# A Nyström block with inverses in one chain, changed to two chains of inverses with a shorter beginning

## The chip, the core and the metric

The kernel runs on one core of a Trainium2 chip. The core has TensorE (PE, matmuls; the weight loads are listed apart as PEld), VectorE (DVE), ScalarE (ACT), GpSimd (POOL) and SyncE (SP, which issues DMAs). Matmuls write to PSUM; DVE and ACT empty it. The metric is the device time of one execution in microseconds (us), lower is better.

## The reference

Sixteen batches of 1024 rows of 256 go through a Nyström attention (16 heads of width 16, 64 landmarks) and then an expert network, each with a layer norm before it, one behind it, and a residual.

```python
def iterative_inv(K, n_iter=6):
    denom = jnp.max(jnp.sum(K, axis=-2), axis=-1)[:, :, None, None]
    V = jnp.swapaxes(K, -1, -2) / denom
    for _ in range(n_iter):
        KV = jnp.matmul(K, V)
        V = jnp.matmul(0.25 * V, 13 * I - jnp.matmul(KV, 15 * I - jnp.matmul(KV, 7 * I - KV)))
    return V
...
Q_l, K_l = means of Q and K over each 16 rows          # 64 landmarks
kernel1 = softmax(Q @ K_l.T); kernel2 = softmax(Q_l @ K_l.T); kernel3 = softmax(Q_l @ K.T)
SV = (kernel1 @ iterative_inv(kernel2)) @ (kernel3 @ V);  out = SV @ w_proj
...
base = x @ W_base + b_base
h = relu(x @ Wd1[e] + bd1[e]);  recon = h @ Wd2[e] + bd2[e]      # 8 experts
idx = argmin over e of mean((recon - x) ** 2)
out = base + relu(x @ Wa_down[idx] + ba_down[idx]) @ Wa_up[idx] + ba_up[idx]
```

kernel2 is a 64x64 matrix per head; its inverse is the iteration above, a long chain of small products. All arithmetic is float32.

## The kernel before

The work of a batch is cut into stages. Stage a (`stage_a`, L322) transposes the normalized rows, makes Q, K and V (L351, L372), the landmark means `lm` (L392) and `bd` (L395; the means of a pair of heads side by side, zero elsewhere), then the weights of kernel3 (L420, L444, L455), their product with V (L483), normalized to `u` (L536). Stage p (`stage_p`, L540) makes kernel2, inverts it and multiplies the inverse with `u` into `w_bd` (L733, L735). Stage c (`stage_c`, L740) makes the weights of kernel1 (L766, L795, L804, L812), multiplies them with `w_bd` (L833), projects (L881) and writes x1. Stage d1 (`stage_d1`, L932) norms x1, runs the eight experts (L954, L987; differences `df` at L995, their squares on ACT at L998), picks the best one and gathers its weights by DMA; stage d2 (`stage_d2`, L1061) computes the output (L1070, L1088, L1089).

Stage p in detail. Eight tiles of 64 columns on 128 partitions hold the 16 matrices. `kp` (L596, four DVE instructions) is the landmark means with all but one pair of heads masked to zero, by `pairmask`; two products of 256 columns with all 128 rows give the scores `pk` (L600). Maximum, difference, exp, sum, reciprocal and product (L608 to L617) make kernel2. A product with `eye` transposes it (L577, `pkt`), L625 sums its columns (`cs`). A transpose of `cs` (L628, `pcs`), maximum and reciprocal over 8 partitions (L630, L632), a copy `rrow` (L634), a transpose back (L637, `prd`) and a copy (`rd`, L639) bring each head's reciprocal denominator to all of its partitions, and `vi` (L641) is the first V. Of the six iterations every second one (0, 2, 4) begins with a product `pkv` of kernel2 and `vi`, each has `psq`, `pb` and a last product (`px` or `pvi`), all made by the helper `product` at L577, 64x64 pieces, 32 records for 16 heads and one product; each step waits for DVE or ACT to turn the step before into the next operand (L653, L655, L692, L698, L662, L683, L707, L723, L725). In iteration 0 a second product with `eye` gives the transposed copy `vt` of `vi` (L577, `pkv<-eye,vi`, and L686). `across` (L658) copies half of the operand y to the other 64 partitions.

The order of the work is not that of the code. Each stage is a generator that yields, before each piece of work, a name, the names that it follows, and the estimated costs on PE, DVE and ACT. Four streams, one per stage kind, each go through the batches 0 to 15 in turn: a, p, c, d1 with d2. A planner (`planned`, L1244) puts the pieces of all streams in one order by a model of the engines: at each point it tries each stream's next piece, looks 70 us ahead (250 us from the end it looks to the end) by simple rules, and takes what loses the least PE time. The rules prefer the stream with the lowest progress: its rank (0 for a, 1 for p, 2 for c, 3 for d) plus the share of its work done, times 16. The order is then fixed for PE, ACT, DVE and POOL; each of them works through its own queue in that order.

What ties the streams: p needs `bd` of its batch; the `bd` step of a (which overwrites `lm`, one buffer) follows `kp` of the batch before; `weighted` of c follows the end of p; Q has three buffers, so a follows c three batches earlier; x1 has two, so c follows d two batches earlier; `u` and `w_bd` have two each. The tiles of p (`mat`, L550) have one buffer each. PSUM is four slots of two banks (`two_banks`, `one_bank` both take one slot), shared by all streams. Large work tiles come from `buf4k` (L106): `df` has three buffers of tag `df`, the normed rows `xn_d` (L942) and the output y_d (L301) two of tag `yd`. The two bias rows that are loaded at the start lie in buffers of `df`. In stage d2 POOL sets three rows of `a_t` (L1065, L1066), issued between the step `a`'s go-ahead and its products.

## Time and profile before

| | |
|---|---|
| median of 10 executions | 2368.16 us (2363.08 to 2371.74) |
| profiled execution, its own time | 2364.72 us |
| its span, first to last instruction | 2362.9 us |
| granted TensorE clock, mean | 0.98 |
| PE, DVE, ACT busy | 2162.4, 1424.4, 1317.1 us |
| DMA | 60.36 MB, 26 GB/s on average |

In a line of groups, "x512" is the count, "238.2, 608" the union of busy time in us and the mean duration in ns of one, and behind the bar stands the idle time of the engine just before these instructions with what ended it; "issue" means that the trace shows nothing that was waited for. PE's records overlap each other, so count times mean is more than busy time. In a line of waits the three numbers are the total, the number of times and the longest, in us. In a line of stretches come the stretch, its length, the busy time of PE, PEld, DVE, ACT and POOL with counts, the granted clock as a share of full speed, the DMA share and GB/s.

### The profile page before, as it was taken

How to read it: one execution, taken by the hardware profiler on the slowest of the kernel's cores; microseconds unless marked ns; L12 is line 12 of the kernel's file. 1: busy time of each engine (PE TensorE's matmuls, PEld its weight loads, DVE VectorE, ACT ScalarE, POOL GpSimd, SP SyncE). 2: the span in 40 equal slices, each digit the busy share in tenths (PEclk: the TensorE clock that was granted, in tenths of full speed). 3: DMA queues.
4: the chain of work that ended last, by engine and by line, in shares of the span. 5: the costliest groups of instructions: out<-in, count | busy, mean ns of one | idle time of the engine just before them, and what ended most of it. 6: DMA issues, size and time to landing. Idle time of an engine off the chain costs nothing.

```text
span 2362.9 us, 85848 instructions
## 1 busy us (share of the span) xinstructions
PE 2162.4 (92%) x39346; PEld 1382.3 (58%) x39346; DVE 1424.4 (60%) x2715; ACT 1317.1 (56%) x2659; POOL 271.7 (12%) x387
## 2 busy tenths in 40 slices
PE   7999989999899999999999999999999999898965
PEld 4666565565655656566565656657556465655442
DVE  6546565756457666666656657575656656474633
ACT  2345655645655556564656646575554655666635
POOL 1001020110200202010020201102010020101021
PEclk9999999999999999999999999999999999999978
DMA  3000001010010100101010100101001010000000
GB/s 112 20 21 21 2 22 39 5 56 2 14 46 3 58 3 16 44 5 56 2 58 2 37 23 3 57 2 59 1 5 56 2 40 2 14 29 24 18 21 21
DMA packets 56626, 60.36 MB, mean 26 GB/s; under 512 B 4996, under 2 KB 55240, under 8 KB 56264
## 3 DMA queue, kind: packets, MB, share of 16 engines
q1 hardware_dynamic: 50240, 50.35, 6.8%
q8 instruction: 309, 5.06, 0.9%
q0 software_dynamic: 2560, 2.14, 0.3%
q10 hardware_dynamic: 3464, 2.37, 0.3%
q14 instruction: 53, 0.43, 0.1%
HBM read 38.08 MB, written 16.78 MB: 23 GB/s over the span
## 4 chain that ended last, share of the span: by engine, by line
PE 43%; DVE 8%; ACT 7%; issue 3%; POOL 1%; DMA 0%; POOLq 0%; DVEq 0%; ACTq 0%
PE ph L954 6%; PE pq L351 5%; PE pr L987 4%; PE pf L1088 4%; PE po L881 3%; ACT df L998 3%; PE pf L1089 2%; DVE df L995 2%; PE pv L372 2%; PE psv L833 2%; PE psct L804 2%; PE psct L812 1%; PE put L483 1%; PE psm L420 1%; PE pb L577 1%
## 5 line engine op out<-in xcount | busy, mean ns | idle before, releaser
L998 ACT ACTIVATE df<-df,bd_sb 128x512 f32<-128x512 f32 x512 | 363.2, 711 | 128.9 <-DVE df L995 128.0
L995 DVE TENSOR_TENSOR df<-pr,xt_d 128x1024 f32<-128x1024 f32 x256 | 302.7, 1217 | 85.0 <-PE pr L987 50.4
L987 PE MATMUL pr<-ht,wd_sb 64*64 64x512 f32 x2048 | 252.3, 597 | 6.7 <-ACT e L822 2.4
L954 PE MATMUL ph<-xt_d,wd_sb 128*128 128x512 f32 x512 | 238.2, 608 | 1.0 <-ACT e L822 0.7
L351 PE MATMUL pq<-xt_a,wqkv_sb 128*128 128x512 f32 x512 | 230.0, 599 | 0.0
L429 DVE TENSOR_REDUCE mx<-psm 128x2 f32<-128x1024 f32 x128 | 149.9, 1216 | 46.2 <-PE psm L420 45.9
L774 DVE TENSOR_REDUCE maxima<-psc 128x16 f32<-128x1024 f32 x128 | 150.1, 1215 | 28.0 <-PE psc L766 28.0
L954 PEld LDWEIGHTS ph<-xt_d,wd_sb 128*128 128x128 f32 x512 | 93.7, 192 | 115.9 <-issue 97.8
L822 ACT ACTIVATE e<-psct 128x1024 f32<-128x1024 f32 x128 | 123.4, 1015 | 66.2 <-PE psct L812 64.3
L351 PEld LDWEIGHTS pq<-xt_a,wqkv_sb 128*128 128x128 f32 x512 | 94.2, 190 | 108.2 <-issue 102.6
L465 ACT ACTIVATE e<-psc 128x1024 f32<-128x1024 f32 x128 | 122.5, 1021 | 32.4 <-PE psc L455 32.2
L1088 PE MATMUL pf<-wbase_sb,xt_d 128*128 128x256 f32 x512 | 137.6, 392 | 1.3 <-ACT xx L683 1.3
L881 PE MATMUL po<-wproj_sb,svt 128*128 128x256 f32 x512 | 120.6, 389 | 7.2 <-ACT vt L707 3.6
L260 POOL TENSOR_SCALAR ve_c_y<-ss_c 128x4 f32<-128x4 f32 x32 | 6.2, 194 | 1023.6 <-ACT square_c L306 1023.3
L692 DVE TENSOR_TENSOR sq<-psq,eye 128x512 f32<-128x512 f32 x96 | 65.8, 686 | 94.3 <-PE psq L577 90.9
L295 DVE SCALAR_TENSOR_TENSOR y_d<-y_d,rstd_d_y,x 128x256 f32<-128x256 f32 x128 | 53.2, 479 | 110.7 <-POOL rstd_d_y L262 110.7
L698 DVE TENSOR_TENSOR t<-eye,pb 128x512 f32<-128x512 f32 x96 | 65.4, 681 | 89.7 <-PE pb L577 89.5
L987 PEld LDWEIGHTS pr<-ht,wd_sb 64*64 64x64 f32 x2048 | 64.6, 133 | 89.3 <-issue 47.9
L372 PE MATMUL pv<-wqkv_sb,xt_a 128*128 128x256 f32 x512 | 116.6, 382 | 0.2 <-ACT e L822 0.2
L962 ACT ACTIVATE ht<-ph,bd_sb 128x1024 f32<-128x1024 f32 x64 | 70.9, 1108 | 74.8 <-PE ph L954 74.4
L881 PEld LDWEIGHTS po<-wproj_sb,svt 128*128 128x128 f32 x512 | 96.5, 193 | 25.9 <-ACT svt L856 4.8
L1088 PEld LDWEIGHTS pf<-wbase_sb,xt_d 128*128 128x128 f32 x512 | 97.9, 194 | 18.5 <-issue 3.4
(183 smaller groups left out, 4118.4 us busy)
## 6 DMA issues: line engine op xcount, KB each, us to landing
out_dram<-y_d SPq DMA_DIRECT2D x32, 512.0 KB
x<-in_L_attn_x_dram SPq DMA_DIRECT2D x15, 1024.0 KB
xa<-in_L_attn_x_dram SPq DMA_DIRECT2D x15, 1024.0 KB
xa<-in_L_attn_x_dram SPq DMA_DIRECT2D x2, 512.0 KB
x<-in_L_attn_x_dram SPq DMA_DIRECT2D x2, 512.0 KB
wqkv_sb<-in_L_attn_w_qkv_dram ACTq DMA_DIRECT2D x1, 768.0 KB
wd_sb<-in_L_ffn_Wd_dram ACTq DMA_DIRECT2D x2, 256.0 KB
wd_sb<-in_L_ffn_Wd_dram ACTq DMA_DIRECT2D x1, 512.0 KB
```

The source lines that it names most:

```text
L351: nc.tensor.matmul(pq[:, n, :], lhsT=wqkv_sb[:, k, f0 : f0 + P], rhs=xt[:, k, n * 512 : (n + 1) * 512], start=(k == 0), stop=(k == NC - 1),)
L372: nc.tensor.matmul(pv[:, j, :], lhsT=xt[:, k, (t0 + j) * P : (t0 + j + 1) * P], rhs=wqkv_sb[:, k, 2 * D : 3 * D], start=(k == 0), stop=(k ...
L429: nc.vector.tensor_reduce(mx3[:, n, q : q + 2], psc[g], X, ALU.max)
L465: nc.scalar.activation(e, psc[g], AF.Exp)
L774: nc.vector.tensor_reduce(mx[:, t0 : t0 + 2, 64 * g : 64 * g + 64].rearrange("x t (p j) -> x p t j", p=2)[:, :, :, 0 : 2 * NC], psc[g].rea ...
L822: nc.scalar.activation(e, psc[g], AF.Exp)
L881: nc.tensor.matmul(po[:, j, :], lhsT=svt[n][:, c, j * P : (j + 1) * P], rhs=wproj_sb[:, c, :], start=(c == 0), stop=(c == NC - 1),)
L954: nc.tensor.matmul(ph[:, n, :], lhsT=wd1_sb[:, k, 2 * i : 2 * i + 2, :].rearrange("p e h -> p (e h)"), rhs=xt[:, k, n * 512 : (n + 1) * 51 ...
L987: nc.tensor.matmul(pr[to, r, :], lhsT=wd2_sb[half, i, k * P + 64 * f : k * P + 64 * f + 64], rhs=ht[half, cols], start=True, stop=True,)
L995: nc.vector.tensor_tensor(df, pr, middle(xt[:, k, cols], 2), ALU.subtract)
L998: nc.scalar.activation(df[:, r, :], df[:, r, :], AF.Square, bias=bd2_sb[:, e, k : k + 1], accum_out=part[:, e, k * NW + n : k * NW + n + 1],)
L1088: nc.tensor.matmul(po[:, j, :], lhsT=xt[:, k, cols], rhs=wbase_sb[:, k, :], start=(k == 0), stop=False)
```

## The change

Stage p begins differently. Each pair of heads has its scores from a product of 32 rows and 64 columns, straight from `lm` (no `kp`, no `pairmask`), into four PSUM banks, two slots; maximum and difference are done for each slot. One product of kernel2 with `in_half` (ones in each 64x64 diagonal block) gives the sums of the columns on every partition of a head; maximum and reciprocal follow directly, `rd` needs no transposes. V in the transposed layout, `vt`, is kernel2 times `rd`; `vi` isn't made, since the first `pkv` is the product of kernel2's transpose with itself, scaled by `rd` on DVE as `xh`, and y is made from `xh`. `across` stores only the half that is read.

Stage p is split into two streams, for even and odd batches, both of rank 1, and its tiles have one buffer for each parity. A stream's progress is now its rank plus the batch plus the done share of that batch. `bd` follows the step `k2` instead of `kp`. `xn_d`, `df` and `y_d` share one pool of four buffers (tag `yd`); the bias rows lie in buffers of `e1`, and stage c of batch 0 follows their use. The memsets of `a_t` are issued in the last step of d1.

```diff
@@ -133,9 +133,9 @@
     nc.scalar.dma_start(out=wbase_sb, in_=w_base.rearrange("(k p) f -> p k f", p=P))
-    bd1_rows = work.tile([E // 2, P], F32, tag="df", name="bd1_rows", bufs=3)
+    bd1_rows = work.tile([E // 2, P], F32, tag="e1", name="bd1_rows")
     nc.scalar.dma_start(out=bd1_rows, in_=bd1.rearrange("(i r) h -> i (r h)", r=2))
-    bd2_rows = work.tile([E * NC, P], F32, tag="df", name="bd2_rows", bufs=3)
+    bd2_rows = work.tile([E * NC, P], F32, tag="e1", name="bd2_rows")
@@ -156,6 +156,10 @@
     nc.gpsimd.memset(ones, 1.0)
+    in_half = const.tile([P, P], F32, name="in_half")
+    nc.gpsimd.memset(in_half, 0.0)
+    for _, half in halves():
+        nc.gpsimd.memset(in_half[half, half], 1.0)
@@ -165,7 +169,6 @@
-    pairmask = groups("pairmask", PC)
@@ -298,7 +301,7 @@
-        y = buf4k(tag, [P, 4, D], f"y_{at}{b}_{h}")
+        y = buf4k(tag, [P, 4, D], f"y_{at}{b}_{h}", 4 if tag == "yd" else 2)
@@ -383,7 +386,7 @@
                     ("a", b, "bd"),
-                    [("a", b, "qk", i, c) for i in range(2) for c in range(NC)] + ([("p", b - 1, "kp")] if b >= 1 else []),
+                    [("a", b, "qk", i, c) for i in range(2) for c in range(NC)] + ([("p", b - 1, "k2")] if b >= 1 else []),
@@ -548,7 +551,7 @@
         def mat(tag, name=None):
-            return inv.tile([P, NP, M], F32, tag=tag, name=f"{name or tag}_{b}")
+            return inv.tile([P, NP, M], F32, tag=f"{tag}{b % 2}", name=f"{name or tag}_{b}")
@@ -573,7 +576,11 @@
                         assert rows_y == rows
-                        yt = y[h[y_at[0]] ^ h[y[2]]] if isinstance(y, tuple) else y
+                        yt = y
+                        if isinstance(y, tuple) and h[y_at[0]] != h[y[2]]:
+                            yt, j = y[1], 2 * (j // 4) + j % 2
+                        elif isinstance(y, tuple):
+                            yt = y[0]
@@ -588,58 +595,60 @@
-        yield step("kp", ew("dve", 0.8, None))
+        yield step(
+            "k2",
+            mm(0.15, "r32", 16),
+            mm(0.15, "r32", 16),
+            *(ew("dve", 0.4, 1) for _ in range(3)),
+            ew("dve", 0.4, 1, "free"),
+            ew("act", 0.5, -1, "free"),
+        )
         lm, bd = live[b].pop("lm"), live[b]["bd"]
-        kp = inv.tile([P, NC, PC, M], F32, tag="yx", name=f"kp_{b}")
-        for p in range(PC):
-            nc.vector.tensor_scalar(kp[:, :, p, :], lm[:, 1], pairmask[:, p : p + 1], None, ALU.mult)
-        yield step("k2", mm(1.3, "full", 8), ew("dve", 1.25, -1, "free"), ew("act", 0.5))
-        pk = one_bank([P, NP, M], f"pk_{b}")
+        pk = [two_banks([P, 2, 512], f"pk_{b}_{g}") for g in range(PC // 2)]
         for c in range(NC):
-            nc.tensor.matmul(
-                pk[:, c * PC : (c + 1) * PC, :].rearrange("x p l -> x (p l)"),
-                lhsT=bd[:, c, :, :].rearrange("f r l -> f (r l)"),
-                rhs=kp[:, c].rearrange("f p l -> f (p l)"),
-                start=True,
-                stop=True,
-            )
-        mx = small.tile([P, NP], F32, tag="mx2", name=f"mx2_{b}", bufs=1)
-        nc.vector.tensor_reduce(mx, pk, X, ALU.max)
+            for p in range(PC):
+                nc.tensor.matmul(
+                    pk[p // 2][:, p % 2, c * M : (c + 1) * M],
+                    lhsT=bd[rows32(p), c, :, :].rearrange("f r l -> f (r l)"),
+                    rhs=lm[rows32(p), 1, c, :],
+                    start=True,
+                    stop=True,
+                )
+        mx = small.tile([P, NP], F32, tag=f"mx2{b % 2}", name=f"mx2_{b}", bufs=1)
         k2 = mat("vt", "k2")
-        nc.vector.tensor_tensor(k2, pk, last(mx, M), ALU.subtract)
+        for g in range(PC // 2):
+            scores = pk[g][:, :, 0 : NC * M].rearrange("x p (c m) -> x p c m", c=NC)
+            most = mx.rearrange("x (c g p) -> x g p c", c=NC, g=2)[:, g]
+            nc.vector.tensor_reduce(most, scores, X, ALU.max)
+            nc.vector.tensor_tensor(
+                k2.rearrange("x (c g p) m -> x g p c m", c=NC, g=2)[:, g], scores, last(most, M), ALU.subtract
+            )
...
         yield step("k2n", ew("dve", 1.5, None))
-        sm = small.tile([P, NP], F32, tag="sm2", name=f"sm2_{b}", bufs=1)
+        sm = small.tile([P, NP], F32, tag=f"sm2{b % 2}", name=f"sm2_{b}", bufs=1)
         nc.vector.tensor_reduce(sm, k2, X, ALU.add)
-        rs = small.tile([P, NP], F32, tag="rs2", name=f"rs2_{b}", bufs=1)
+        rs = small.tile([P, NP], F32, tag=f"rs2{b % 2}", name=f"rs2_{b}", bufs=1)
...
         nc.vector.tensor_tensor(k2, k2, last(rs, M), ALU.mult)
-        yield step("k2t", mm(Q, "q64", 64), ew("act", 0.5, -1, "free"), ew("dve", 0.6))
...
+        yield step(
+            "k2t", mm(0.9, "full", 4), mm(Q, "q64", 64), ew("dve", 0.85, 0, "free"), ew("act", 0.5, 1, "free"), ew("dve", 0.6, None, "aside")
+        )
+        pcs = one_bank([P, NP, M], f"pcs_{b}")
+        nc.tensor.matmul(
+            pcs.rearrange("x q m -> x (q m)"), lhsT=in_half, rhs=k2.rearrange("x q m -> x (q m)"), start=True, stop=True
+        )
...
         kt_at = product(pkt[0], (k2, NATURAL), (eye, None), "t", ("p2", "s"))
+        cs = small.tile([P, NP], F32, tag=f"cs{b % 2}", name=f"cs_{b}", bufs=1)
+        nc.vector.tensor_reduce(cs, pcs, X, ALU.max)
+        rd = small.tile([P, NP], F32, tag=f"rd{b % 2}", name=f"rd_{b}", bufs=1)
+        nc.vector.reciprocal(rd, cs)
...
-        cs = small.tile([P, NP], F32, tag="cs", name=f"cs_{b}", bufs=1)
-        nc.vector.tensor_reduce(cs, k2t, X, ALU.add)
-        yield step("rrow", mm(0.2, "full", 4), ew("dve", 0.6, -1, "free"))
-        pcs = one_bank([NP, 2, M], f"pcs_{b}")
-        nc.tensor.transpose(pcs.rearrange("q r m -> q (r m)"), cs, ident)
-        cmx = small.tile([NP, 2], F32, tag="cmx", name=f"cmx_{b}", bufs=1)
-        nc.vector.tensor_reduce(cmx, pcs, X, ALU.max)
-        rmx = small.tile([NP, 2], F32, tag="rmx", name=f"rmx_{b}", bufs=1)
-        nc.vector.reciprocal(rmx, cmx)
-        rrow = inv.tile([NP, 2, M], F32, tag="yc", name=f"rrow_{b}")
-        nc.vector.tensor_copy(rrow, last(rmx, M))
-        yield step("v0", mm(0.1, "full", 2), ew("act", 0.15, -1, "free"), ew("dve", 0.6))
-        prd = one_bank([P, NP], f"prd_{b}")
-        nc.tensor.transpose(prd, rrow.rearrange("q r m -> q (r m)"), ident[:NP, :NP])
-        rd = small.tile([P, NP], F32, tag="rd", name=f"rd_{b}", bufs=1)
-        nc.scalar.copy(rd, prd)
-        vi = mat("vi")
-        nc.vector.tensor_tensor(vi, k2t, last(rd, M), ALU.mult)
-        v_at = kt_at
+        vt, vt_at = k2, NATURAL
+        nc.vector.tensor_tensor(vt, k2, last(rd, M), ALU.mult)
@@ -656,34 +665,36 @@
         def across(y):
-            other = mat("yc", "across")
-            frm, to = (t.rearrange("x (f k p) m -> x f k (p m)", f=2, k=2) for t in (y, other))
+            other = inv.tile([P, NP // 2, M], F32, tag=f"yc{b % 2}", name=f"across_{b}")
+            frm, to = y.rearrange("x (f k p) m -> x f k (p m)", f=2, k=2), other.rearrange("x (f p) m -> x f (p m)", f=2)
             for r, half in halves():
-                nc.scalar.copy(to[64 - 64 * r : 128 - 64 * r, :, r, :], frm[half, :, 1 - r, :])
+                nc.scalar.copy(to[64 - 64 * r : 128 - 64 * r], frm[half, :, 1 - r, :])
...
             if i % 2 == 0:
-                n = 2 if i == 0 else 1
...
                     f"kv{i}",
-                    mm(n * Q, "q64", 64 * n),
-                    ew("dve", 0.6, 0),
-                    ew("act", 0.5, 0, "aside" if i == 0 else "free aside"),
-                    *([ew("act", 0.5, 0, "free aside")] if i == 0 else []),
+                    mm(Q, "q64", 64),
+                    ew("dve", 0.6, 0, "free" if i == 0 else ""),
+                    ew("dve", 0.6) if i == 0 else ew("act", 0.5, 0, "free aside"),
...
                 )
-                px, pvt = banks_of(f"pkv{i}")
-                x_at = product(px, (k2t, kt_at), (vi, v_at), h, (g, "p2"))
+                px, _ = banks_of(f"pkv{i}")
+                first = (k2t, kt_at) if i == 0 else (vi, v_at)
+                x_at = product(px, (k2t, kt_at), first, h, (g, "p2"))
                 if i == 0:
-                    vt_at = product(pvt, (vi, v_at), (eye, None), h, (g, "p2"))
-                y = taken_y(px, 1.0)
-                xh = mat("xx")
-                nc.scalar.copy(xh, px)
-                if i == 0:
-                    vt = mat("vt")
-                    nc.scalar.copy(vt, pvt)
+                    xh, y = mat("xx"), mat("yx")
+                    by_pair, rd_by_pair = px.rearrange("x (u p) m -> x u p m", p=2), rd.rearrange("x (p u) -> x u p", p=2)
+                    nc.vector.tensor_tensor(
+                        xh.rearrange("x (u p) m -> x u p m", p=2), by_pair, last(rd_by_pair, M), ALU.mult
+                    )
+                    nc.vector.tensor_tensor(y, xh, middle(eyes[0], NP), ALU.subtract)
+                else:
+                    y = taken_y(px, 1.0)
+                    xh = mat("xx")
+                    nc.scalar.copy(xh, px)
@@ -741,7 +752,7 @@
         w_bd = w_bds[b % 2]
-        first = [("a", b, "bd"), *([("d", b - 2, "end")] if b >= 2 else [])]
+        first = [("a", b, "bd"), *([("d", 0, "weights")] if b == 0 else []), *([("d", b - 2, "end")] if b >= 2 else [])]
@@ -939,7 +950,7 @@
         def dst(h):
-            xns[h] = buf4k("yd", [P, 4, D], f"xn_d{b}_{h}")
+            xns[h] = buf4k("yd", [P, 4, D], f"xn_d{b}_{h}", 4)
@@ -991,7 +1002,7 @@
                             )
-                    df = buf4k("df", [P, 2, 512], f"df_{b}_{i}_{k}_{n}", 3)
+                    df = buf4k("yd", [P, 2, 512], f"df_{b}_{i}_{k}_{n}", 4)
@@ -1056,14 +1067,14 @@
         centre(wup)
-        live[b].update(xt=xt, wdn=wdn, bdn=bdn, wup=wup)
...
-    def stage_d2(b):
-        xt, wdn, bdn, wup, x1 = (live[b].pop(k) for k in ("xt", "wdn", "bdn", "wup", "x1"))
-        yield go(("d", b, "a"), [("d", b, "wup")], mm(1.72, "c64", 16), ew("act", 1.0, -1, "free"))
...
         nc.gpsimd.memset(a_t[R : R + 2, :], 0.5)
+        live[b].update(xt=xt, wdn=wdn, bdn=bdn, wup=wup, a_t=a_t)
...
+    def stage_d2(b):
+        xt, wdn, bdn, wup, x1, a_t = (live[b].pop(k) for k in ("xt", "wdn", "bdn", "wup", "x1", "a_t"))
+        yield go(("d", b, "a"), [("d", b, "wup")], mm(1.72, "c64", 16), ew("act", 1.0, -1, "free"))
@@ -1098,15 +1109,21 @@
-    def chain(stages):
-        for b in range(NB):
+    def chain(stages, batches=range(NB)):
+        for b in batches:
...
-    RANKS = 0, 1, 2, 3
+    RANKS = 0, 1, 1, 2, 3
     def streams():
-        return [chain(stages) for stages in ([stage_a], [stage_p], [stage_c], [stage_d1, stage_d2])]
+        return [
+            chain([stage_a]),
+            chain([stage_p], range(0, NB, 2)),
+            chain([stage_p], range(1, NB, 2)),
+            chain([stage_c]),
+            chain([stage_d1, stage_d2]),
+        ]
@@ -1123,11 +1140,17 @@
     for rank, stream in zip(RANKS, stretches):
-        sums = [0.0]
-        for _, _, parts in stream:
-            sums.append(sums[-1] + sum(p[1] for p in parts if p[0] == "pe"))
+        sums, of_batch = [0.0], [0.0] * (NB + 1)
+        at, stream_progress = {}, []
+        for (_, b, *_), _, parts in stream:
+            of_batch[b] += sum(p[1] for p in parts if p[0] == "pe")
+        for (_, b, *_), _, parts in stream:
+            us = sum(p[1] for p in parts if p[0] == "pe")
+            at[b] = at.get(b, 0.0) + us
+            stream_progress.append(rank + b + (at[b] - us) / max(of_batch[b], 1.0))
+            sums.append(sums[-1] + us)
         before.append(sums)
-        progress.append([rank + NB * at / sums[-1] for at in sums])
+        progress.append(stream_progress)
...

```

## The prediction

> **What bounds the kernel now.** I read the page's totals first, then TensorE's groups by shape, then TensorE's waits, then the order in time around one inverse, then the last quarter millisecond in stretches.
>
> The page's totals, before:
>
> ```profile
> span 2362.9 us, 85848 instructions
> PE 2162.4 (92%) x39346; PEld 1382.3 (58%) x39346; DVE 1424.4 (60%) x2715; ACT 1317.1 (56%) x2659; POOL 271.7 (12%) x387
> ```
>
> TensorE (PE) is the bound; VectorE (DVE) and ScalarE (ACT) have 40% of their time free. So a microsecond of PE work is worth about a microsecond, work on the others is worth something only where PE waits for it. PE's groups by shape (busy us, mean ns | idle before):
>
> ```profile
> L954 PE MATMUL ph<-xt_d,wd_sb 128*128 128x512 f32 x512 | 238.2, 608 | 1.0 <-ACT e L822 0.7
> L766 PE MATMUL psc<-bd,qt 32*128 32x128 f32 x2048 | 81.7, 285 | 5.6 <-DVE t L698 2.3 <-DVE mx L429 1.3 <-DVE maxima L774 0.6
> L577 PE MATMUL psq<-yx 64*64 64x64 f32 x3072 | 67.7, 224 | 11.4 <-DVE yx L653 4.4 <-DVE yx L655 1.9 <-issue 1.8
> L577 PE MATMUL pb<-yx,sq 64*64 64x64 f32 x1536 | 65.3, 223 | 16.4 <-DVE sq L692 8.8 <-ACT e L822 6.3 <-ACT vt L707 0.6
> L577 PE MATMUL pkv<-vi,k2t 64*64 64x64 f32 x1536 | 34.9, 228 | 5.6 <-issue 2.6 <-ACT vi L723 2.1 <-DVE vi L641 0.6
> L600 PE MATMUL pk<-kp,bd 128*128 128x256 f32 x64 | 17.6, 397 | 1.2 <-DVE kp L596 0.7 <-DVE u L536 0.3 <-ACT e L822 0.2
> L577 PE MATMUL pkv<-eye,vi 64*64 64x64 f32 x512 | 11.1, 221 | 1.9 <-issue 1.9
> L628 PE MATMUL pcs<-ident,cs 128*8 128x128 f32 x16 | 4.4, 272 | 3.4 <-DVE cs L625 3.4
> L637 PE MATMUL prd<-ident,rrow 8*128 8x8 f32 x16 | 3.3, 208 | 0.5 <-DVE df L995 0.4
> ```
>
> Matmuls overlap, so the price of one is busy time over count, not the mean: 0.465 us for L954's 512 columns. Each product in the code leaves two records, a transpose one. PE's waits, the rows that matter here:
>
> ```profile
> PE pb L577 <- DVE sq L692: 8.8, 10, 1.8
> PE pf L1089 <- POOL a_t L1066: 8.3, 5, 3.8
> PE pb L577 <- ACT e L822: 6.3, 7, 1.8
> PE psq L577 <- DVE yx L653: 4.4, 5, 1.7
> PE po L881 <- ACT vt L707: 3.6, 2, 2.0
> ```
>
> The first and fourth are the inverse waiting for its own last step. The third and fifth are another thing: pb reads no e, so there PE waited for a PSUM slot that ScalarE was emptying. DVE's order in time where one inverse gives way to the next (start, us):
>
> ```profile
> 1244.66 0.86 DVE L596 TENSOR_SCALAR kp<-lm,pairmask 128x128 f32<-128x128 f32 x4
> 1245.56 0.29 DVE L392 TENSOR_SCALAR lm<-lsum 128x256 f32<-128x256 f32 x1
> ...
> 1264.81 0.69 DVE L641 TENSOR_TENSOR vi<-k2t,rd 128x512 f32<-128x512 f32 x1 [4.34 <-ACT rd L639]
> ```
>
> kp of batch 9 (counted from 0) is followed at once by lm of batch 10: stage a of the next batch stood ready and waited for an inverse to begin, and an inverse begins when the one before ends. The instructions of kp run from 38.3 (first) to 2082.9 (last of 16 batches), (2082.9 - 38.3) / 15 = 136 us apart, while one inverse takes 159.8 - 38.3 = 121 us (first) and 2184.3 - 2082.9 = 101 us (last) from kp to its product pw. The one chain of inverses is nearly always under way. The end, in stretches (PE busy, granted clock after POOL):
>
> ```profile
> 2140.00:2170.00 30.00, 23.34 (x490) 17.29 (x485) 10.94 (x31) 13.90 (x31) 7.92 (x9) 0.94 0.03 7
> 2170.00:2200.00 30.00, 23.21 (x476) 18.32 (x476) 17.91 (x41) 12.68 (x29) 4.81 (x8) 0.83 0.22 72
> 2230.00:2264.00 34.00, 26.22 (x381) 14.04 (x379) 16.14 (x36) 22.15 (x53) 7.30 (x9) 0.89 0.02 6
> ```
>
> **The change part by part.** The sum is against the profiled execution, 2364.7 us (span 2362.9), 3.4 below the median of ten, 2368.2.
>
> *PE work out.* pk 17.6 + the transposed copy of vi 11.1 + pcs 4.4 + prd 3.3 = 36.4 us, all on PE.
>
> *PE work in.* The product with in_half has 512 columns, one per batch, 32 records at L954's 0.465 = 14.9 us. The scores by pairs are 8 products of 64 columns on 32 rows per batch, 256 records. L766 (32 rows, 128 columns) costs 81.7 / 2048 = 0.040, so at most 10.2; by half the columns 5.1; by 64-column pkv, 34.9 / 1536 = 0.023, 5.8. I take 6, since pkv has the same columns. Net -36.4 + 20.9 = -15.5 (ends -11 and -16). The Trainium skill, "TensorEngine Tiling (Array Packing)", section Restrictions and Gotchas, speaks against this part: row tiles need different PSUM banks at the same time, so the step holds more PSUM. The code does hold two slots of four where pk held one; by the rule the step's gain of 11.6 (17.6 - 6) would be given back in waits, a sum of 2326.
>
> *Steps out.* The two visits of PE for pcs and prd go with their waits, 3.4 + 0.5, and the 1.2 before pk is traded for a like wait: -4 (ends 0 and -7).
>
> *VectorE and ScalarE.* Out on DVE: kp 13.8, cmx 4.4, rmx 2.4, rrow 3.4 = 24.0. In: rd 16 x 0.203 = 3.2; xh by a multiplication 16 x 0.686 = 11.0; maxima and subtraction in halves, 64 of 0.419 (L493, 128x256) = 26.8 for 22.1 now. Net -5. ACT loses rd 2.6, vt 9.5 and 16 xx copies of 0.583 = 21.4. Both lie beside PE's work: 0. Where the cover is gone, in the chain of one inverse, kp to vi took 1264.81 + 0.69 - 1244.66 = 20.8 us; kp (0.86), the rrow operations (0.27 + 0.15 + 0.21) and the wait for rd (4.34) go, xh before y adds 0.69, so about 5 us per inverse, which only the chain feels.
>
> *Two streams.* The idle before all L577 groups except the removed one sums to 11.4 + 16.4 + 2.7 + 5.6 + 4.4 + 0.8 + 6.5 + 7.0 + 1.3 = 56.1 us. In it 14.6 are "issue", which stays, and about 10.5 waits for a PSUM slot; 31 are waits of one inverse for itself. With the other inverse at another step these have cover: ends 0 (both always wait together) and -31. I take -18, some three fifths, because another chain is close behind: stage c of a batch waits for stage d two batches earlier (x1 has two buffers), and stage c and d of one batch span about 261 us (batch 9: from its first scores at 1376 to its last output at 1637), 131 per batch against the inverse's 136. PE's idle is 2362.9 - 2162.4 = 200.5 us, 12 of it after its last matmul (2351); before other products it is thus 132. Start (14.5), last batch (11.2 + 5.3 + 7.9), a_t (8.3), issue (about 22) and the steps out (7) leave 56, of which a further ready product may fill a seventh: -8 (ends 0 and -56).
>
> *Against that.* Two inverses hold PSUM slots while the engines empty them. The waits for slots in PE's list sum to about 45 us over the span; I add a quarter, +10 (ends 0 and +70, the rival).
>
> *The end.* In 2140 to 2264 PE is busy 23.3 + 23.2 + 29.7 + 26.2 = 102.5 of 124, idle 21.5; the clock's missing shares (0.06 x 30 + 0.17 x 30 + 0.11 x 34) are 10.6 more. In that time the last inverse is alone on its chain and ends at 2185, though its bd was written at 1958 and the stage c before ended at 2163. With two streams it is done before. But stage c of batch 15 also waits for stage d of batch 13, which ends at 2182, so that is what is late next. I take -8 (ends 0 and -32). After 2264 stage d of the last batch is alone, ScalarE's squares bound it: 0.
>
> *Clock.* From 300 to 1800 the missing shares of the 100 us stretches sum to about 17 us, after short idles. With a third of the idle gone: -5 (ends 0 and -17). The Trainium skill, "TensorE: Matmul & The Clock Gate", section HAM oscillation, gives as its rule to have no idle gaps above about 3.4 us. The trace has no gap over 2 us in 2170 to 2200 and 0.83 there, so the row is followed; by the rule this term would be 0 and the sum 5 higher.
>
> *a_t.* Its two memsets (0.94 us each, one of 3.4) are issued a step earlier, behind the gathers on POOL's queue, and no longer between PE's pad and pf: -6 of 8.3 (ends 0 and -8.3). Queued behind them on POOL are the norms' rstd, at most 1.9 us later, whose users wait for DVE and ACT anyway. Next late is wup (1.4).
>
> *One pool of buffers.* xn, df and y take 20 tiles per batch in turn from four buffers, instead of two and three. df has four at its disposal where it had three, so the 13.0 us that DVE waited for ACT df may shrink; y's write to HBM has a batch's norms before its buffer returns. DVE isn't the bound: 0 (ends -3 and +3). bias rows earlier and in_half's three memsets: under 1 us in the start: 0.
>
> Sum: -15.5 - 4 - 18 - 8 + 10 - 8 - 5 - 6 = -54.5, which is 2310 for the profiled execution and, with 3.4 added, **2314 us** for the median.
>
> **The rivals.**
> *The second inverse finds no use* (the change doesn't do what it says). Each step's number rises by one with the batch, so the planner may keep the later inverse back until the earlier has ended, as now, or the chain of c and d sets the pace. PE's 92% speaks for it, the 31 us of waits against. Then only the work, the steps and a_t count: 2368.2 - (15.5 + 4 + 6 = 25.5) = 2343 us.
> *It fills nearly all.* All 31, half of the 56, 21 at the end, 12 of clock, no PSUM price, with the 25.5: -117.5, 2251 us. For it: stage a is freed from the inverse too (lm waits only for the scores). Against: slots.
> *PSUM becomes the limit, slower.* Four slots; a step holds one from its first product until the engine has emptied it, the scores two. Steps are about 21 + 2 per batch, 368 in all. The gains without the +10 are 64.5, so at 64.5 / 368 = 0.18 us of added wait per step they are gone; at 0.25 us it is 92, 2396 us. For it: 45 us of slot waits already; against: they are spread over many places, the largest 6.3 us in 7 times.
>
> **How the numbers follow.** Forecast (2285 to 2335) 0.42, no use (2335 to 2363) 0.21, fills nearly all (2230 to 2285) 0.19, slower 0.14; within 0.2%, about what a measurement of this kernel tells from no change, 0.04. Faster is 0.42 + 0.21 + 0.19 = 0.82. The range of 8 in 10 leaves out the lower part of the third and the upper of the fourth, some 0.09 each: 2250 to 2380. The likeliest case's own is 2285 to 2335.
>
> **What would show it.** PE's busy time near 2147; mx of a batch begun over 60 us before pw of the batch before (right), or after it (no use). The idle before L577's groups near 38 (56 - 18); the row pf <- POOL a_t gone; waits for slots near 55. The last inverse ended before 2120. I am wrong if the slot waits double or more, or if idle moves to another stream's products, those of c and d first.

## The result, and the profile after

The changed kernel takes 2351.85 us (median of 15 executions, 2345.85 to 2364.8) against 2367.12 us of the kernel before beside it: ratio 0.9942, 95% interval 0.993 to 0.9954. That is faster by 0.6%, some 14 us, where 54 were forecast and 2250 to 2380 us was the range. The direction was right, the size was a quarter. The profiled execution of the changed kernel took 2359.5 us and is one of its slower ones, at a mean clock of 0.974; its others lay between 0.973 (2364.8 us) and 0.981 (2345.9 us). The kernel before itself took 2361 to 2367 us on some occasions and 2432 to 2436 us on others, so below only ratios to it, run beside, are compared, and traces only within one such condition.

The page's totals, after:

```profile
span 2357.7 us, 84960 instructions
PE 2173.8 (92%) x39026; PEld 1393.4 (59%) x39026; DVE 1413.4 (60%) x2666; ACT 1299.5 (55%) x2611; POOL 273.8 (12%) x390
```

PE has 320 records fewer, and its busy time is 11.4 us longer; 2147 was expected. Its idle time fell from 200.5 to 183.9 us. PE's groups by shape, after:

```profile
L584 PE MATMUL psq<-yx 64*64 64x64 f32 x3072 | 66.4, 224 | 7.3 <-ACT vt L718 2.2 <-DVE yx L662 1.6 <-ACT e L468 1.2
L584 PE MATMUL pb<-yx,sq 64*64 64x64 f32 x1536 | 66.1, 226 | 6.8 <-DVE sq L703 4.3 <-ACT vt L718 0.8 <-ACT e L833 0.8
L638 PE MATMUL pcs<-k,in_half 128*128 128x512 f32 x32 | 17.4, 624 | 1.3 <-ACT xx L697 1.3
L610 PE MATMUL pk<-lm,bd 32*128 32x64 f32 x256 | 15.0, 293 | 3.5 <-DVE mx L432 2.0 <-DVE df L1006 0.7 <-ACT mt L808 0.6
```

The idle before psq fell from 11.4 to 7.3, before pb from 16.4 to 6.8; all groups of the helper (now L584) together wait 37.4 us, and 38 were expected. But pk costs 15.0 us, not 6. PE's waits, after, and below them two rows of before that the prediction didn't show:

```profile
PE psv L844 <- issue: 16.5, 15, 2.1
PE put L486 <- issue: 9.6, 6, 2.3
PE pb L584 <- DVE sq L703: 4.3, 7, 0.9
PE pf L1100 <- POOL a_t L1072: 3.8, 1, 3.8
```

```profile
PE psv L833 <- issue: 11.2, 10, 2.0
PE put L483 <- issue: 6.6, 8, 2.3
```

The inverse waits for its sq half as long, and the waits that the trace gives no cause for ("issue") have grown. The wait for a_t that is left is the one of the last batch. The two inverses do overlap. DVE's order in time has the beginning of batch 8's inverse, PE's the last product of batch 7's, 111 us later:

```profile
988.68 0.43 DVE L622 TENSOR_REDUCE mx<-pk 128x4 f32<-128x256 f32 x1 [5.55 <-PE pk L610]
```

```profile
1099.54 1.89 PE L744 MATMUL pw<-u,vt 64*64 64x16 f32 x32
```

Over the batches this lead is 34 to 118 us, more than 60 in ten cases of 15. An inverse now takes 115 to 231 us from the transposition of kernel2 to pw, 174 on the mean, where it took 91 to 144, 119 on the mean: two go side by side for part of their way, each at about two thirds of the pace. The end, in the stretches shown for before (PE busy first, granted clock after POOL):

```profile
2140.00:2170.00 30.00, 27.26 (x450) 19.96 (x444) 8.70 (x26) 16.50 (x38) 9.14 (x11) 0.97 0.03 7
2170.00:2200.00 30.00, 25.30 (x476) 18.07 (x476) 20.55 (x46) 10.77 (x21) 5.14 (x8) 0.83 0.23 72
2230.00:2264.00 34.00, 25.62 (x384) 14.77 (x377) 15.17 (x34) 18.95 (x43) 7.93 (x9) 0.86 0.02 6
```

The last inverse ends at 2186 us, where it ended at 2185, and the clock still drops. PE's idle time from 2140 to 2264 us is 16.1 us, where it was 21.5.

For the whole span the two profiled executions can be set against each other with the trace's clock records: 94.9 us at half clock before, 125.7 after (2 us of each lie behind the last instruction). Counting half-clock time as half, PE's work is 2162.4 - 94.9 / 2 = 2115.0 us before and 2173.8 - 125.7 / 2 = 2110.9 after. So the 5.2 us between them are -4.1 of work, +15.4 of clock and -16.5 of idle. (In some 29 us of the half-clock time of each PE stood idle; that lowers both figures of work alike.) The +15.4 belongs to these two executions and not to the kernels: over 17 executions the changed kernel's mean clock is 0.977, and over 23 and 17 executions of the kernel before on two other occasions at the same speed (beside e13 to e16, and beside e17 and e18) it is 0.978 and 0.977. Side by side, in e5, both have 0.964 (11 and 28 executions). If the clocks were as alike beside each other here, which the record doesn't have for before, the 15 us between the medians are work and idle.

### The profile page after: what moved, and what is told of

The parts are those of the page before. It is cut to its first block, busy times and chain, and to the rows that moved or that the text cites. A ratio compares the mean times of both kernels' runs of the same rounds, so it can differ in the third digit from the quotient of the medians.

```text
span 2357.7 us, 84960 instructions
## 1 busy us (share of the span) xinstructions
PE 2173.8 (92%) x39026; PEld 1393.4 (59%) x39026; DVE 1413.4 (60%) x2666; ACT 1299.5 (55%) x2611; POOL 273.8 (12%) x390
## 3 DMA queue, kind: packets, MB, share of 16 engines
q8 instruction: 306, 5.01, 0.9%
## 4 chain that ended last, share of the span: by engine, by line
PE 71%; DVE 13%; ACT 11%; issue 4%; POOL 1%; DMA 1%; POOLq 0%; DVEq 0%; SPq 0%; ACTq 0%
PE pq L354 9%; PE ph L965 9%; PE pr L998 6%; PE pv L375 5%; PE pf L1099 5%; PE po L892 4%; ACT df L1009 4%; PE psv L844 3%; PE psct L815 3%; DVE mx L432 3%; DVE df L1006 2%; PE pf L1100 2%; PE psc L777 2%; PE psm L423 2%; PE psc L447 2%
## 5 line engine op out<-in xcount | busy, mean ns | idle before, releaser
L844 PE MATMUL psv<-w_bd,e 128*32 128x34 f32 x8192 | 90.5, 199 | 21.8 <-issue 16.5
L844 PEld LDWEIGHTS psv<-w_bd,e 128*32 128x32 f32 x8192 | 80.4, 110 | 48.7 <-issue 27.0
L375 PEld LDWEIGHTS pv<-wqkv_sb,xt_a 128*128 128x128 f32 x512 | 95.7, 190 | 19.1 <-issue 4.1
```

The lines of the kernel that those rows point to most:

```text
L375: nc.tensor.matmul(pv[:, j, :], lhsT=xt[:, k, (t0 + j) * P : (t0 + j + 1) * P], rhs=wqkv_sb[:, k, 2 * D : 3 * D], start=(k == 0), stop=(k ...
L844: nc.tensor.matmul(psv[rows32(g), j // 2, col : col + 2 * (HD + 1)], lhsT=es[p // 2][:, p % 2, j * P + 32 * g : j * P + 32 * g + 32], rhs= ...
```

## The experiments

The ratios are to the kernel before, run beside each.

I began with theory A (the second stream gives its gain, the new beginning next to nothing), rival B (the reverse), and C (the planner's order itself moves the time).

**e1: two streams, old beginning.** The kernel before with everything of the change but the new beginning of the inverse.

```diff
-    RANKS = 0, 1, 2, 3
+    RANKS = 0, 1, 1, 2, 3
+            chain([stage_p], range(0, NB, 2)),
+            chain([stage_p], range(1, NB, 2)),
...
-            return inv.tile([P, NP, M], F32, tag=tag, name=f"{name or tag}_{b}")
+            return inv.tile([P, NP, M], F32, tag=f"{tag}{b % 2}", name=f"{name or tag}_{b}")
```

> The kernel before with two streams of inverses (tiles by parity, new progress, one pool of buffers, a_t early), but the old beginning of the inverse (kp, pk, transposes). Theory A (the second stream gives its 18 us of waits of the inverse for itself, the new beginning gives next to nothing, since its products cost nearly what they replace: 15.0 + 17.4 us of busy time in for 36.4 out): ratio to before 0.993 to 0.997, near the whole change's 0.994. Rival B (the new beginning gives its 15 us as forecast and the second stream costs what it gains): 0.999 to 1.003.

Measured: 0.9929 (0.9906 to 0.9952).

**e2: one stream, new beginning.** The changed kernel with the two lines of the inverse's streams made one.

```diff
-    RANKS = 0, 1, 1, 2, 3
+    RANKS = 0, 1, 2, 3
-            chain([stage_p], range(0, NB, 2)),
-            chain([stage_p], range(1, NB, 2)),
+            chain([stage_p]),
```

> The changed kernel with one stream of inverses, all else of the change kept (new beginning, pool, a_t early). Theory A: 0.997 to 1.001 of before (4 us of work and 4 of a_t, 8 us or less). Rival B: 0.990 to 0.994, as good as or better than the whole change. Rival C (any new order of the work moves the time by some 10 us, whatever the change): both this and the run with two streams alone may lie anywhere within 0.99 to 1.005, and do not add up.

Measured: 0.9886 (0.9862 to 0.9909). Each half alone is as fast as or faster than the whole. e1 lies at the edge of A's range, e2 below B's range and just below C's. A and B can't both be read from that; it is nearest to what C describes.

**e3: only the pool and a_t**, in before's order of the work.

```diff
-                    df = buf4k("df", [P, 2, 512], f"df_{b}_{i}_{k}_{n}", 3)
+                    df = buf4k("yd", [P, 2, 512], f"df_{b}_{i}_{k}_{n}", 4)
...
         centre(wup)
+        a_t = work.tile([R + 3, N], F32, tag="ht", name=f"a_t_{b}")
+        nc.gpsimd.memset(a_t[R : R + 3, :], 1.0)
+        nc.gpsimd.memset(a_t[R : R + 2, :], 0.5)
```

> The kernel before with the one pool of four buffers for xn, df and y and with a_t's memsets a step earlier, nothing else; the planner knows neither, so the order of the work is that of before, except for the two memsets. Forecast's steps (a_t -6, pool 0): ratio 0.9965 to 0.998. If the early memsets only move the wait to the next thing (wup, the gathers): 0.999 to 1.000. If sharing the buffers costs: above 1.001.

Measured: 0.9979 (0.9962 to 0.9996), 5 us, as forecast in sum. The wait itself went only from 8.3 to 6.7 us, so part of the 5 comes from elsewhere or from the noise (the interval is 1 to 9 us); what, I can't say.

**e4: the scores twice.** The loop over the eight score products is run twice over the same place, in the changed kernel's order.

```diff
-        for c in range(NC):
+        for c in [*range(NC), *range(NC)]:
```

> The changed kernel with the eight score products of each batch issued twice into the same place (the second time overwrites the first), in the same order of the work: 256 more records on PE. If a record of 32x64 costs what the 64-column pieces of the inverse cost in a stream (0.023 us), PE's busy time rises by 6 us and the time by 4 to 8 us over the changed kernel: then the 15.0 us that pk costs are mostly a fixed cost of a short visit, (15.0 - 6) / 16 = 0.56 us each. If each record costs 15.0 / 256 = 0.059, it rises by 13 to 17 us: then the products themselves were priced too low.

Measured: 1.0019 (0.9999 to 1.0039), against 0.9955 of the changed kernel (e5), 15 us more. The group's line in e4, then in e5:

```profile
L610 PE MATMUL pk<-lm,bd 32*128 32x64 f32 x512 | 24.0, 294 | 5.7 <-DVE mx L432 2.2 <-ACT mt L808 1.6 <-ACT vt L718 0.8
```

```profile
L610 PE MATMUL pk<-lm,bd 32*128 32x64 f32 x256 | 15.8, 300 | 3.7 <-DVE mx L432 2.0 <-DVE df L1006 0.7 <-ACT mt L808 0.6
```

256 more records cost 24.0 - 15.8 = 8.2 us, 0.032 each; so of the 15.8 us of one set, 7.6 are a fixed 0.48 us for each of the 16 visits. The price by streaming rows that the prediction used has no such part. The other half of the 15 us is not in this group: half-clock time in e4 is 214.3 us against 193.9, worth 10 us, and the mean clock over the executions is 0.957 against 0.964. By the group's line the first expectation (a fixed cost per visit) holds; by PE's whole busy time (2227.9 against 2212.8 us) and by the time the second would, but both contain the clock. I follow the group.

**e5 to e8: the same work in another order.** e5 is the changed kernel again. e6, e7 and e8 set the planner's look-ahead to 76 us in the changed kernel, in the kernel before and in the kernel of e2.

```diff
-AHEAD, LAST, GAP = 70.0, 250.0, 1.0
+AHEAD, LAST, GAP = 76.0, 250.0, 1.0
```

> The changed kernel unaltered, to stand beside the following three on one chip. Expected as measured first: 0.993 to 0.9955 of before.

> The changed kernel with the planner's look-ahead set to 76 us instead of 70: the same work, buffers and dependencies, another order. Theory C (the greedy planner's order is itself worth some 10 us either way, so that a change's ratio of half a percent says little of its parts): the ratio to before differs by 0.002 to 0.008 from the changed kernel's. Theory D (the order is settled by the dependencies and the parts of the change have each their own worth): within 0.0015 of the changed kernel.

> The kernel before with the look-ahead at 76 us. Theory C: 0.992 to 1.008, off 1 by 0.002 or more. Theory D: 0.9985 to 1.0015.

> The changed kernel with one stream of inverses (which gave 0.9886) with the look-ahead at 76 us. Theory C: back towards the changed kernel, 0.991 to 0.998. Theory D: 0.987 to 0.990, and the second stream costs what separates it from the changed kernel.

Measured: 0.9955 (0.9937 to 0.9973), 0.9968 (0.9951 to 0.9984), 1.0091 (1.0069 to 1.0114), 0.9996 (0.9979 to 1.0013). Before and one stream move by 0.9% and 1.1% with nothing but the order changed, more than even C allowed for, so D falls. The changed kernel moved by 0.13% only, as D said; C stands for the other two.

**e9 and e10: the planner told of slower instructions**, in the changed kernel and in before.

```diff
-BLOCK, FETCH = 256, 3.4
+BLOCK, FETCH = 256, 4.6
```

> The changed kernel, with the planner told that a block of 256 PE instructions takes 4.6 us to arrive instead of 3.4; work, buffers and dependencies unchanged. Theory E (the waits without a cause in the trace, called issue, are PE waiting for its next block of instructions, and orders with dense short products pay for them twice, by the wait and by the halved clock after it): waits on issue fall below 55 us (82.1 in the changed kernel on the second chip, 47.3 on the first), half-clock time below 160 us (193.9), ratio to before 0.985 to 0.992. If the planner can't steer these waits: within 0.993 to 0.999, waits on issue as before.

> The kernel before with the same setting, 4.6 us. Theory E: its waits on issue fall from 66 to below 55 us too, ratio 0.988 to 0.996. Theory C alone (any other order): 0.992 to 1.010 without a relation to these waits.

Measured: 0.9917 (0.9899 to 0.9934) and 1.007 (1.0044 to 1.0096). Waits on issue went from 82.1 (e5) to 63.9 us in the changed kernel, not below 55, half-clock time from 193.9 to 187; in before they stayed at 65.8 (66.4 in e3). The longest such row, e5 and then e9:

```profile
PE psv L844 <- issue: 32.1, 45, 2.3
```

```profile
PE psv L844 <- issue: 19.4, 36, 1.6
```

The ratio of e9 lies in theory E's range, but neither of its two signs came, e10 went the other way, and e6, another order without this setting, waits only 58.6 us on issue. That the setting steers these waits, and isn't one more draw of the order, is not shown.

**e11 and e12: is the chain of c and d through x1 next?** e11 gives x1 three buffers, paid for by two instead of four for xn, df and y; e12 has only the smaller pool, in the changed kernel's order.

```diff
-        first = [("a", b, "bd"), *([("d", 0, "weights")] if b == 0 else []), *([("d", b - 2, "end")] if b >= 2 else [])]
+        first = [("a", b, "bd"), *([("d", 0, "weights")] if b == 0 else []), *([("d", b - 3, "end")] if b >= 3 else [])]
...
-        load(b, "x1", 2)
+        load(b, "x1", 3)
...
-                    df = buf4k("yd", [P, 2, 512], f"df_{b}_{i}_{k}_{n}", 4)
+                    df = buf4k("yd", [P, 2, 512], f"df_{b}_{i}_{k}_{n}", 2)
```

> The changed kernel with three buffers of x1, so that stage c of a batch waits for stage d three batches earlier instead of two; to make room, xn, df and y share two buffers instead of four. Theory F (the chain of stages c and d through x1 is what paces the run once the inverses are free; in the changed kernel's trace stage c of batches 11, 12 and 13 begins 2, 2 and 1 us after stage d two batches before has ended): PE's waits for a stage's own data other than the inverse's (29.8 us) and for slots (36.2) fall by 20 us or more in sum, ratio at least 0.006 below the next kernel's. Otherwise, PE's own pace or the order decides: within 0.005 of it, either sign.

> The changed kernel with two buffers instead of four for xn, df and y, in the same order of the work; what the pool of four is worth, and the base for the kernel with three x1. Forecast's step (the pool is worth 0, DVE being off the bound): ratio 0.9945 to 0.9975, as the changed kernel's 0.9955. If df needs the buffers: above 1.000.

Measured: 1.0022 (1.0005 to 1.0039) and 1.0011 (0.9995 to 1.0027). In e11 stage c did get ahead: PE's order has the first scores of batch 11, DVE's the end of stage d of batch 9 only 30 us later:

```profile
1704.64 1.07 PE L777 MATMUL psc<-bd,qt 32*128 32x128 f32 x32
```

```profile
1734.27 1.66 DVE L298 SCALAR_TENSOR_TENSOR y_d<-y_d,rstd_d_y,x 128x256 f32<-128x256 f32 x4
```

It gained nothing: waits for a slot and for other products' operands are no shorter in sum than in e12. F's 0.006 did not come. Since the new ties also draw a new order, and a draw moves the time by more than that (below), this speaks against F and against the reason that the prediction gave for its cautious 18 us, but one order does not exclude a smaller gain. e12 also shows what the pool is worth: against e5's 0.9955, two buffers cost 0.56%, 13 us. DVE waits for ACT's squares 55 times instead of 5 (e12, then e5):

```profile
DVE df L1006 <- ACT df L1009: 24.1, 55, 1.9
```

```profile
DVE df L1006 <- ACT df L1009: 10.9, 5, 2.9
```

**e13 to e18: more orders**, of two streams (e13 with 64 us, e16 with 82 us), of one (e14 with 64, e17 with 82, e18 told 4.6 us for a block) and of before (e15 with 64). The edits are those of e6 and e9 with these numbers.

> The changed kernel with the look-ahead at 64 us: a third order of the same work (fourth with the run told of slower blocks). If the second stream is worth its 17 us on the mean over orders: 0.985 to 0.990 on the mean of changed and 0.008 below one stream. If its gain is given back in waits elsewhere: within 0.991 to 0.999, PE's waits of the inverse for itself 12 to 25 us, its waits on issue plus half the half-clock time 10 us or more above one stream's.

> The changed kernel with one stream of inverses, look-ahead at 64 us: a third order of it (0.9886 at 70, 0.9996 at 76). If the second stream gains nothing on the mean: 0.988 to 1.000, waits of the inverse for itself 30 to 45 us. If it gains 17 us: above 1.000.

> The kernel before with the look-ahead at 64 us: a fourth order of it (1.000, 1.0091, 1.007). If the shown order of before is a lucky one among its own: 1.003 to 1.010. If not: 0.992 to 1.000.

> The changed kernel with the look-ahead at 82 us: one more order. Expected as the other orders of it: 0.990 to 0.999 of before.

> The changed kernel with one stream of inverses, look-ahead at 82 us, a fourth order. Two streams gave 0.9949 (mean of two measurements), 0.9968, 0.9917, 0.9907 and 0.9916 in five orders, mean 0.993; one stream 0.9886, 0.9996 and 1.0018, mean 0.997. If the second stream is worth about 10 us of its 18: this and the next lie at 0.995 to 1.002. If it is worth nothing: around 0.993, 0.988 to 0.997.

> The changed kernel with one stream of inverses and the planner told 4.6 us for a block of instructions, a fifth order. As for the run with 82 us: 0.995 to 1.002 if the second stream is worth about 10 us, 0.988 to 0.997 if nothing. Its waits of the inverse for itself: 28 to 43 us, as in the other orders of one stream.

Measured: e13 0.9907 (0.9886 to 0.9928), e14 1.0018 (1.0003 to 1.0032), e15 0.9979 (0.9959 to 0.9998), e16 0.9916 (0.9891 to 0.9941), e17 0.9874 (0.9854 to 0.9893), e18 1.0029 (1.0014 to 1.0044).

e13, e15 and e16 lie near or in what was expected of one more order; e15 lies in the range for a shown order of before that is not lucky. e14 lies above 1, the range for a second stream that gains 17 us. e17 and e18 lie below and above every range that was stated for them.

All orders, each with its ratio and, in us, worked out from its trace: PE's work (busy time less half of the half-clock time), half-clock time, and PE's idle by what ended it: on issue, the inverse's products waiting for an operand, other products waiting for an operand (without the four long waits of the start and the last batch, 35 to 37 us in each), and waits for an engine that the product reads nothing of (a PSUM slot). Each row is one execution. PE stood idle in part of the half-clock time, which makes the column of work 13 to 27 us too low; that spreads by some 7 us within each half of the table.

| kernel | ratio | work | half clock | issue | inverse | others | slot |
|---|---|---|---|---|---|---|---|
| *before at 2361 to 2367 us* | | | | | | | |
| before, 70 | 1 | 2115.0 | 94.9 | 38.9 | 28.3 | 31.9 | 47.9 |
| before, 64 (e15) | 0.9979 | 2125.2 | 91.5 | 32.4 | 26.0 | 27.5 | 42.1 |
| changed, 70 | 0.9942 | 2110.9 | 125.7 | 47.3 | 11.1 | 29.3 | 43.4 |
| changed, 64 (e13) | 0.9907 | 2109.6 | 104.9 | 39.3 | 21.0 | 26.6 | 34.5 |
| changed, 82 (e16) | 0.9916 | 2113.5 | 88.1 | 41.1 | 17.6 | 27.5 | 44.0 |
| one stream, 64 (e14) | 1.0018 | 2105.3 | 113.5 | 34.9 | 30.0 | 35.4 | 48.7 |
| one stream, 82 (e17) | 0.9874 | 2113.6 | 78.0 | 33.0 | 23.3 | 25.3 | 40.0 |
| one stream, told 4.6 (e18) | 1.0029 | 2125.0 | 98.8 | 33.0 | 36.2 | 28.2 | 46.0 |
| *before at 2432 to 2436 us* | | | | | | | |
| changed, 70 (e5) | 0.9955 | 2115.9 | 193.9 | 82.1 | 12.0 | 29.8 | 36.2 |
| changed, 76 (e6) | 0.9968 | 2111.8 | 164.7 | 58.6 | 24.4 | 33.8 | 51.0 |
| changed, told 4.6 (e9) | 0.9917 | 2116.8 | 187.0 | 63.9 | 18.8 | 28.2 | 47.3 |
| one stream, 70 (e2) | 0.9886 | 2107.3 | 153.7 | 65.9 | 34.2 | 21.3 | 44.8 |
| one stream, 76 (e8) | 0.9996 | 2110.7 | 186.9 | 62.8 | 43.4 | 21.6 | 44.2 |
| before, 76 (e7) | 1.0091 | 2109.4 | 217.6 | 73.2 | 30.6 | 29.8 | 50.7 |
| before, told 4.6 (e10) | 1.007 | 2132.0 | 190.3 | 65.8 | 34.3 | 28.9 | 44.1 |

Over its orders (the changed kernel at 70 counted once, with the mean of its two measurements) two streams have a mean ratio of 0.993 (spread 0.003, five orders), one stream 0.996 (0.007, five), before 1.0035 (0.005, four). So the change as a whole is worth about 1.0% on the mean over orders (uncertain by 0.3%), 25 us. The order of before that the forecast took as base may be on the lucky side of its own: two of three others are slower, e15 is not. The two streams against one are 0.003 apart with an uncertainty of 0.0035: whether the second stream gains anything is not settled. What it does to the inverse is seen in both halves of the table. The inverse's waits fall by 13 us (16.6 against 29.8 on the mean) and by 20 us (18.4 against 38.8). Waits on issue are higher by 9 and 4 us, and half-clock time by 9 and 12 us, worth 5 and 6. In these executions that takes back 14 of 13 and 10 of 20. But the orders of one kernel differ by more than this in the slower half (58.6 to 82.1 us on issue), and by the mean clock over all executions the part of the clock is only 1 to 2 us. What eats the gain is thus not shown; the other columns move either way.

e17, one stream with the look-ahead at 82 us, took 2333.3 us beside 2365.5 of before, and is faster than both kernels: its interval ends at 0.9893, that of the changed kernel begins at 0.993. Its page's totals:

```profile
span 2326.9 us, 85073 instructions
PE 2152.6 (93%) x39026; PEld 1381.8 (59%) x39026; DVE 1415.4 (61%) x2666; ACT 1302.4 (56%) x2611; POOL 272.5 (12%) x390
```

Its inverse waits 23.3 us, the least of one stream, and it has the least time at half clock. That e18, the same kernel in an order planned with other constants, is 1.6% slower says that this is an order found by chance and no property of one stream.

## Why the prediction was wrong

The terms are set against the two profiled executions, where work and idle time fell by 20.6 us and the forecast had 49.5 for them.

**PE work (-15.5): mis-sized, -4.0.** By groups, 36.4 us went and 15.0 + 17.4 came. The scores were taken at 6 us, by the 64-column pieces that stream in long sequences; a visit of 16 records has a fixed 0.48 us (e4), so eight of these microseconds are paid for coming at all. The end of the range taken from the nearest 32-row group, 10.2, was nearer, and still too low. pcs has L954's columns and costs 0.54 us a record instead of 0.465, perhaps because a lone product has no neighbour to overlap with; no run tests that. The objection of the Trainium skill's page "TensorEngine Tiling (Array Packing)" to this step, PSUM pressure, did not show: slot waits fell from 47.9 to 43.4 us.

**Two streams (-18): right in its place, wrong for the sum.** The helper's idle fell by 18.7. But the 8 us at other products didn't come: PE's idle elsewhere, 142.5 us before without the removed copy, is 146.5 after. Waits on issue rose by 8.4 us (38.9 to 47.3). That a shorter wait of the inverse lets PE run through short records faster, and so into these waits, is a reading that no run tests. The prediction held the streams' gain down because stage c and d of one batch took 131 us against the inverse's 136. It read the start of batch 9's stage c as 1376 us; its first scores are earlier:

```profile
1356.75 1.10 PE L766 MATMUL psc<-bd,qt 32*128 32x128 f32 x30
```

With batch 9's last output at 1637, c and d took 280 us, 140 for each batch by the two buffers of x1, so this chain was no faster than the inverse's.

**Against that, slots (+10): no price**, -4.5. Over the five orders of two streams slot waits are 34.5 to 51.0 us, over those of before 42.1 to 50.7. The slower rival's mechanism never appeared.

**The end (-8): not by its mechanism.** With a partner at its side the last inverse took 140 us instead of 91 and ended at the same time, where the prediction had it done before 2120. In this order the two, sharing PE, didn't end earlier than one after the other. PE's idle in that stretch fell by 5.4 us all the same; what did that was not looked into.

**Clock (-5): mis-sized, about 0.** In the profiled pair it is +15.4, which would be the largest single miss, but the changed kernel's profiled execution is one of its slower ones, and over many executions, though of before only on other occasions or in e5, the mean clocks agree within 0.001. I let the loss shrink with the idle time; it did not.

**a_t (-6)**: -4.5 at that wait in the changed kernel, -1.6 in e3, where the sum with the pool was 5. **Steps out (-4)**: the waits of 7.0 us that went were replaced by 4.8 before pk and pcs, -2. **The pool (0)**: e3 shows no cost of four shared buffers against two and three. The reason given, that DVE isn't the bound, does not carry: with two buffers DVE is no more the bound, and they cost 13 us (e12). That the term held was luck.

**The step that failed as a whole** is the sizing of the sum: the work put in was priced at 20.9 us and costs 32.4, and the idle time, forecast to fall by 34 us, fell by 16.5, since only the inverse's own share of it came. Behind the second part lies that one executed order was the base of every idle term. The change gives the planner new pieces, so all of the order is drawn again, and e7, e8, e14, e17 and e18 show what a draw is worth with the same instructions: up to 1.6%, 37 us. The mean over orders, 25 us, puts some 10 of the 40 missing microseconds down to the draw and 11 belong to the work; for the rest the cause stays open. The parts that don't depend on the order were -4 of work and a few microseconds of a_t. The rival *no use*, at 2343 us, was nearest in time, but not in its reason: the second inverse was used.

## What to carry to other kernels

Where a planner sets the order, a small change draws a new order, and its time can't be told from the draw: run the same work in several orders (a look-ahead a few us longer does it) before giving a part of the change its worth. Price short PE steps by visit as well as by record. Compare clocks over many executions, not over two profiled ones. When idle is removed at one place, look whether it comes back at another: here the inverse waited 17 us less, and PE's idle as a whole fell by no more than that.

## What the runs showed of the hardware

**The clock halves mostly after a half-idle step.** The trace's clock records change only in steps of 3.413 us. I cut the profiled executions into these steps. In the kernel before, all 17 halvings came after a step in which PE was busy 57% or less; mid-run the lowest was 0.30 and no gap between products was longer than 2.3 us. Steps above 60% were never followed by one there, some between 45% and 60% were not either. In the changed kernel 21 of 24 came after 59% or less, three after 69 to 74%. Over all twenty traces it is 400 of 478 after 60% or less, and 78 after more, up to fully busy steps in e4 and e18, so this is no complete rule. The Trainium skill, "TensorE: Matmul & The Clock Gate", section HAM oscillation, has as its rule to avoid idle gaps above about 3.4 us; in the kernel before shorter ones, together about half a step, were enough, and each step at half speed, 3.4 us, costs up to 1.7 us. So 1 us of wait beside another can cost more than its length. The executions of the changed kernel between 2346 and 2365 us, with clocks from 0.981 to 0.973, differ by what their time at half clock is worth, 19 us.

**PE waits for its instructions.** The page of the changed kernel lists 306 transfers of the instruction queue with 5.01 MB, 16 KB each; PE's 78052 products and weight loads make 255 for each. The starts of two transfers were seldom closer than 3.5 us (5th percentile), and of the 37 waits on issue over 0.3 us that PE had, the middle one ended 1.38 us after such a block had landed (10th to 90th percentile 1.26 to 1.47, all within 1.2 to 1.6). psv, 128 products and as many weight loads in 1.3 us, waits most. The Trainium skill, "Runtime: NRT & Kernel Launch", section Instruction fetch mechanics, says that crossing such a block is mostly hidden; by count that holds here, 37 waits at 306 blocks, but 32 to 82 us of a span are not hidden, and nearly twice as much of it on the occasions where the kernel before took 2432 us and more (in before's order, e3: 66 us instead of 39). There the link is weaker: in e5 only 39 of 95 such waits ended 1.2 to 1.6 us after a block had landed. What ends the others, and why it differs between occasions, is open.
